# Spare TensorE products in the first two batches, and a re-planned order, in a graph-attention kernel

## The chip, the cores and the metric

The kernel runs on one core of a Trainium2 chip. The metric is the device time of one execution in microseconds. Lower is better. All matrix work is in float32 (some of it in the chip's rounded float32 form for scores).

## The reference

There are 16 batches of 1024 nodes with 256 features and a 1024 x 1024 adjacency of 0 and 1. Each batch goes through two layers, one after the other:

```python
# layer 0: 8 heads of 32
e = einsum('whqd,whkd->whqk', heads(x @ Wq), heads(x @ Wk))
e = where(e >= 0, e, 0.2 * e)
attn = softmax(where(adj > 0, e, NEG), axis=-1)
h = (attn @ heads(x @ Wv)).merge_heads()
o = concat([layernorm(h, g1, b1), x]) @ Wffn.T
x = layernorm(o, g2, b2) + x
# layer 1: two graph attentions, then a feed-forward of 1024
for W, a in ((W1, a1), (W2, a2)):
    Wh = h @ W                                  # h starts as x
    s = leaky_relu(Wh @ a[:256] + (Wh @ a[256:]).T, 0.2)
    h = softmax(where(adj > 0, s, NEG), axis=1) @ Wh
r = layernorm(x + h, g_ln1, b_ln1)
y = layernorm(r + relu(r @ w_ff1 + b_ff1) @ w_ff2 + b_ff2, g_ln2, b_ln2)
```

## The kernel before

**Batches as threads.** Each batch is cut into many small Python generators ("threads"). A thread yields what it needs: an engine for so many nanoseconds (`on`), a buffer of a pool (`take`, `give`), an event (`wait`, `fire`). The class `Order` is a planner that runs when the program is built. It keeps a clock for each engine, picks among the operations that could start within 300 ns (`WINDOW`) the one whose thread has the earliest due time (`aim`), and lets the thread emit the instruction. The order in which instructions are emitted is the order on each engine's queue. Each engine takes its queue strictly in that order, so a plan that is off shows up as waits. The planner also models TensorE's clock: in stretches of 3413 ns, half speed after a stretch that was busy less than 43% (`STRETCH`, `WORK`, `end`).

**Due times.** `SLOT` is the planned time of a batch. `PACE` is the time of two tiles of attention weights. The table `AIM` holds the due times as shares of a slot: when a batch's x, mask and projections come, how fast its heads go (`fast0`, `fast1`, `fast15` for the first, second and last batch; 1 for the others), how far scores may lead (`lead`), and when the rows of the graph layers (`graph`, `graph_step`), the first graph product (`second`), the second one (`normed`) and the feed-forward (`ff`) fall due.

**Layer 0 of a batch.** `project` loads x in four pairs of tiles and turns them (`x_pair`, L351), makes the mask from the adjacency (`mask_part`: DVE at L400, TensorE turns at L409, ACT copies at L413), and projects. `qk_part` computes a half of q or k (L460), splits it into a high and a low part (L463 on ACT, L465 on DVE), and stores both in DRAM through SP's queue (L469). The pool `stage` lets two such parts be in flight. `load_stacks` waits for the four halves of a group of four heads and loads each head's q and k stacks (SP, L543). Then for each head and pair of tiles: scores on TensorE (`all_scores`, L576), scaling by 0.2 on ACT or, in batch 0, DVE (L594, L592), the maximum on DVE (L596), the exponential on ACT (L599), the mask product on POOL (L603), and the product with the values on TensorE (`all_values`, L623). There are 64 such tiles of 128 x 1024 a batch, five buffers `p` and two PSUM buffers for scores.

**The rest of a batch.** `rest` normalizes the heads (L645 to L656, L329 to L345), multiplies with Wffn (L725, L728), and makes the rows of the first graph layer (L757). `attention` makes the graph weights: `first_half` the exponentials of one side, L831 those of the other, `attend` eight rows of 128 x 1024 on DVE (L810, L813) into the one buffer `big`. `second_rows` is the first graph product (L847), `normed_pair` the second (L872, with `as_rows` at L900 adding the residual), `feed_forward` the last stage (L912, L940). The rest of one batch is interleaved with the heads of the next.

**Setup.** `prepare` loads the vectors and small weights through SP's queue, turns and multiplies the weights on TensorE (L1044, L1050), and folds a bias (L1082). Each vector of length 128 c is loaded by `load_cols` (L288) as a tile of 128 partitions and c columns, element by element.

Of the kernel before, what the change touches and what calls it, by code (L numbers as in the profile page):

```python
# [20 lines left out]
P = 128  # L21
# [13 lines left out]
class Order:  # L35
# [18 lines left out]
    def __init__(self, **pools):  # L54
        self.clock = defaultdict(float)
        self.port = 0.0
        self.transfers = 0.0
        self.stretch, self.done, self.half = 0, 0.0, True
        self.pools = {k: [0.0] * n for k, n in pools.items()}
        self.queues = defaultdict(list)  # L60
        self.events = {}
        self.waiting = defaultdict(list)
        self.active = []
        self.made = 0
        self.now = 0.0
        self.busy = defaultdict(float)

    def add(self, thread, aim, ready=0.0):
# [47 lines left out]
    def end(self, engine, t, cost):  # L116
        if engine != "PE":
            return t + cost
        while True:
# [11 lines left out]
            if cost < 0.01:  # L131
                return t

    def run(self):
        while self.active:
            could = []
            for th in self.active:
                costs, shared, delay = th["op"]
                best = None
                for engine, cost in costs.items():  # L140
                    ready = th["ready"]
                    if th.get("last", ())[:2] == (engine, ready):
                        ready -= self.HOP[engine]
                    t = max(self.clock[engine], ready)
                    if shared and engine in ("DVE", "POOL"):
                        t = max(t, self.port)
                    if best is None or t + cost < best[0] + best[2]:
                        best = t, engine, cost
                could.append((best, th))
            first = min(c[0][0] for c in could)  # L150
            (t, engine, cost), th = min((c for c in could if c[0][0] <= first + self.WINDOW),
                                        key=lambda c: (c[1]["aim"], c[1]["no"]))
            if th["op"][1] and engine in ("DVE", "POOL"):

                lead = 100.0 if engine == "DVE" else -100.0
                before = [c for c in could if c[1]["op"][1] and c[0][1] in ("DVE", "POOL")
                          and c[0][1] != engine and c[0][0] + lead < t]
                if before:
                    (t, engine, cost), th = min(before, key=lambda c: (c[1]["aim"], c[1]["no"]))
            costs, shared, delay = th["op"]  # L160
            self.active.remove(th)
            end = self.clock[engine] = self.end(engine, t, cost)
            self.busy[engine] += cost
            if shared and engine in ("DVE", "POOL"):
                self.port = end
            self.now = t
            th["ready"] = end + self.HOP[engine]
            th["last"] = engine, th["ready"]
            if delay:
                self.transfers = max(self.transfers, end + 1000) + 1450 * max(1, round(cost / 500))  # L170
                th["ready"] = max(end + delay, self.transfers + 1200)
                th["last"] = None, 0
            self.step(th, engine)
        stuck = {k: len(v) for k, v in list(self.waiting.items()) + list(self.queues.items()) if v}
        assert not stuck, f"threads that never end: {stuck}"
# [18 lines left out]
def take(pool):  # L194
    return "take", pool
# [29 lines left out]
def unshifted_path(  # L225
# [21 lines left out]
    YW = D + 2  # L247
    NSUM = NT * H + 2 * NT
    NSCORE = 4 * NT
    SLOT = 253e3  # L250
    PACE = SLOT / (H * NT // 2)


    AIM = dict(x=0.818, x_step=0, mask=0.747, mask_step=0.0264, qk0=0.614, qk1=0.898, qk_step=0.0231, v0=0.832,
               v1=0.974, v_step=0.0591, rows=-0.244, rows_step=0.0408, first0=0.12, first1=0.252,
               graph0=-0.009, graph1=0.21, graph_step=0, second=0.355, second_step=0.0335, normed=0.78,
               normed_step=0.026, ff_wait=(None, 0, 1, 0), ff=(0.532, -0.011, 0.487, 0.497), ff_step=0.0386,
               fast0=0.521, fast1=0.85, fast15=0.832, lead=3.15)

    const = ctx.enter_context(tc.tile_pool(name="const", bufs=1))  # L260
    sb = ctx.enter_context(tc.tile_pool(name="sb", bufs=1))
# [21 lines left out]
        nc.sync.dma_start(dst, w.rearrange("(c p) o -> p c o", p=P))  # L283
        return dst

    def load_cols(v, name):
        t = const.tile([P, v.shape[0] // P], FT, name=name)
        nc.sync.dma_start(t, v.rearrange("(c p) -> p c", p=P), allow_slow_non_contiguous=True)  # L288
        return t

    def load_row(v, name):
        t = const.tile([P, v.shape[0]], FT, name=name)
        nc.sync.dma_start(t, bass.AP(tensor=v.tensor, offset=v.offset, ap=[[0, P], [1, v.shape[0]]]))
# [5 lines left out]
    wf2 = const.tile([P, HC, D], FT, name="wf2")  # L299
    w12 = const.tile([P, DC, YW + 2], FT, name="w12")  # L300
    right = const.tile([P, B, 4], FT, name="right")
    k = {}


# [141 lines left out]
    def qk_part(b, g, o, nh):  # L446

        w = (wq, wk)[o]
        cols = slice(nh * HALF, (nh + 1) * HALF)
        for u in range(nh * 2, nh * 2 + 2):  # L450
            yield wait(("xT", b, u))
        yield take("stage")
        yield take("pair")
        yield take("pair")
        yield take("misc")
        pa = misc()
        high, low = (buf([P, HALF], "pair", n) for n in ("high", "low"))
        yield on(PE=1720)
        for dc in range(DC):
            nc.tensor.matmul(pa, w[:, dc, g * P:(g + 1) * P], xTs[b][:, dc, cols],  # L460
                             start=(dc == 0), stop=(dc == DC - 1))
        yield on(ACT=590)
        nc.scalar.copy(high.bitcast(FR), pa)  # L463
        yield on(DVE=690)
        nc.vector.tensor_tensor(low, pa, high, op=OP.subtract)  # L465
        yield give("misc")
        yield load(2)
        for i, part in enumerate((high, low)):
            nc.sync.dma_start(scratch[b, g][o, :, i, cols], part)  # L469
        yield give("pair")  # L470
        yield give("pair")
        yield give("stage")
        yield fire(("qk", b, g, o, nh))

    def project_qk(b, g, t0):
# [130 lines left out]
    def all_values():  # L606
        for b in range(B):
            for h in range(H):
                g, c = h // G, (h % G) * VW
                for u in range(NP):  # L610
                    yield wait(("v", b, g, u))
                v = vs[b, g]
                yield take("acc")
                acc = psum.tile([P, HALF], FT, tag="acc", name="ps_a", bufs=bufs["acc"])
                for d in range(0, NT, GV):
                    for t in range(d, d + GV):
                        yield wait(("p", b, h, t))
                    yield aim(begin[b] + (h * NT + d + 2) / 2 * pace(b), SLOT)
                    yield on(PE=240 + 860 * GV)
                    for t in range(d, d + GV):  # L620
                        p = probs.pop((b, h, t))
                        for nh in range(NH):
                            nc.tensor.matmul(acc[nh * 64:(nh + 1) * 64, :], v[:, t, c:c + 64],  # L623
                                             p[:, nh * HALF:(nh + 1) * HALF],
                                             start=(t == 0), stop=(t == NT - 1))
                    for t in range(GV):
                        yield give("p")
                yield start(after_head(b, h, acc), begin[b] + (h + 1) * NT // 2 * pace(b))
                if h % G == G - 1:
                    yield give("v")  # L630
            yield start(rest(b), work.now)

    def after_head(b, h, acc):
        if h == 0:
# [226 lines left out]
    def normed_pair(b, u, big, y2):  # L861
# [6 lines left out]
        for i, t in enumerate(tiles):  # L868
            for half in range(2):
                yield on(PE=1720)  # L870
                for j in range(half * NT // 2, (half + 1) * NT // 2):
                    nc.tensor.matmul(pa[:, i * D:(i + 1) * D], big[:, j, t * P:(t + 1) * P], y2[:, j, :D],  # L872
                                     start=(j == 0), stop=False)
            yield on(PE=430)
            as_rows(pa, i, x1, i)
        yield fire(("weighed", b, u))
        yield give("pair")
# [48 lines left out]
    def feed_forward(b, u, rT):  # L926
# [9 lines left out]
        for i in range(2):  # L936
            for half in range(2):
                yield on(PE=1720)
                for hc in range(half * HC // 2, (half + 1) * HC // 2):
                    nc.tensor.matmul(pa[:, i * D:(i + 1) * D], hid[hc // 2][:, hc % 2, i * P:(i + 1) * P], wf2[:, hc, :],  # L940
                                     start=(hc == 0), stop=False)
            yield on(PE=430)
            as_rows(pa, i, rT, i)
        for _ in range(HC // 2 + 1):
            yield give("pair")
# [62 lines left out]
    def prepare():  # L1008
# [4 lines left out]
        def part(i, n):  # L1013
            return setup[:, i * 512:i * 512 + DC * n].rearrange("p (c n) -> p c n", c=DC)

        for name, v in (("g1c", g1), ("b1c", b1), ("g2c", g2), ("b2c", b2), ("gl1c", g_ln1), ("bl1c", b_ln1),
                        ("bf1", b_ff1), ("bf2c", b_ff2)):
            yield load(1, 6000)
            k[name] = load_cols(v, name)
        for name, v in (("gl2", g_ln2), ("bl2", b_ln2)):  # L1020
            yield load()
            k[name] = load_row(v, name)
# [24 lines left out]
        def product(wT, dc, by, width):  # L1047
# [3 lines left out]
                                     start=(fc == 0), stop=(fc == DC - 1))  # L1051
            return emit

        for ic in range(2 * DC):
            yield from piece(300, D, wffnT[:, ic, :], flips(wf, ic))
        wTs = []
# [28 lines left out]
        nc.vector.tensor_tensor(k["bf1"], k["bf1"], pa[:, :HC], op=OP.subtract)  # L1085
        yield give("misc")


    with tc.manual_schedule():
        for dst, w in ((wq, Wq), (wk, Wk), (wv, Wv)):  # L1090
            load_w(dst, w)
        work.add(project(0, -SLOT), 0.0)
        work.add(load_stacks(), 0.0)
        work.add(all_scores(), 0.0)
        work.add(all_values(), 0.0)
        work.add(prepare(), 0.5 * SLOT)
        work.run()
# [308 lines left out]
```

## Time and profile before

| | |
|---|---|
| Time of three runs | 4533.11 us in the median, 4531.16 to 4534.94 |
| Profiled span | 4531.4 us, mean granted TensorE clock 0.987 |
| Busy TensorE | 4348.7 us (96%) |
| Busy DVE, ACT, POOL | 3304.5, 2893.6, 2454.6 us |
| L603, mask product on POOL | 1024 of 2177 ns |
| L596, maximum on DVE | 1024 of 1213 ns |
| L623, value products on TensorE | 1019.9 us busy in 4096 |
| L576, scores on TensorE | 631.5 us busy in 2048 |
| L810 and L813, graph rows on DVE | 352.7 and 329.8 us in 256 each |

The profile is one execution. Its busy time of an engine counts the union of that engine's instructions, while the mean of one instruction includes what overlaps with its neighbours; of matmuls, which are pipelined, the busy time divided by the count is the useful figure. A stretch row gives the stretch, its length, the busy time (and number of instructions) of each engine, the TensorE clock granted, and what the DMA engines did.

### The profile page before, as it was taken

The page shows a single profiled execution, that of the slowest core. Times are in us where ns is not written, and L with a number is a line of the kernel's source. Part 1 is how long each engine was busy: PE and PEld are TensorE (multiplying, and loading weights), DVE is VectorE, ACT ScalarE, POOL GpSimd, SP SyncE. Part 2 cuts the span into 40 slices and gives each one's busy share as a digit, 9 for nine tenths or more (in the row PEclk, how much of TensorE's full clock was granted, in tenths as well). Part 3 has the DMA queues.
Part 4 walks back from the last instruction along what each step waited for, and adds up shares of the span by engine and source line. Part 5 has one row for each costly group of instructions (what it writes and reads, how often), then busy time and mean ns, then how long its engine had stood idle before and what let it go on. Part 6 is the DMA issues. An engine that isn't in the chain of part 4 may idle for free.

```text
span 4531.4 us, 57125 instructions
## 1 busy us (share of the span) xinstructions
PE 4348.7 (96%) x20298; PEld 2924.8 (65%) x20298; DVE 3304.5 (73%) x5246; ACT 2893.6 (64%) x4030; POOL 2454.6 (54%) x1544
## 2 busy tenths in 40 slices
PE   6778999999999999999999999999999999999999
PEld 3345666767666676666767666676666767666587
DVE  4766778777787777768777787777768777776854
ACT  4556666666666666666676666666676676666631
POOL 3655565465565545655565565555655565565710
PEclk8899999999999999999999999999999999999999
DMA  5312223222232312323132232322323222231100
GB/s 173 106 49 70 82 70 101 62 79 81 62 98 63 105 54 75 96 59 110 54 89 75 59 98 67 103 64 70 89 64 105 63 86 68 60 99 49 34 22 20
DMA packets 159108, 343.57 MB, mean 76 GB/s; under 512 B 24672, under 2 KB 27232, under 8 KB 158816
## 3 DMA queue, kind: packets, MB, share of 16 engines
q1 hardware_dynamic: 112736, 255.93, 20.0%
q10 hardware_dynamic: 46080, 83.91, 6.2%
q8 instruction: 164, 2.69, 0.2%
q14 instruction: 128, 1.05, 0.1%
HBM read 239.09 MB, written 100.66 MB: 75 GB/s over the span
## 4 chain that ended last, share of the span: by engine, by line
PE 72%; DVE 15%; POOL 5%; issue 4%; ACT 2%; DMA 0%; ACTq 0%; POOLq 0%; SPq 0%; DVEq 0%
PE ps_a L623 16%; PE ps_s L576 10%; PE ps_m L872 8%; PE ps_m L847 8%; PE ps_m L912 7%; PE ps_m L940 7%; DVE att L810 5%; POOL p L603 5%; DVE att L813 5%; PE ps_m L460 3%; DVE p L596 3%; PE ps_m L757 3%; PE ps_m L725 2%; PE ps_m L728 2%; PE ps_m L351 2%
## 5 line engine op out<-in xcount | busy, mean ns | idle before, releaser
L603 POOL TENSOR_TENSOR p<-p,mask 128x1024 f32<-128x1024 f32 x1024 | 2212.3, 2177 | 1654.9 <-ACT p L599 1528.0
L596 DVE TENSOR_TENSOR p<-p,ps_s 128x1024 f32<-128x1024 f32 x1024 | 1209.9, 1213 | 403.0 <-ACT p L594 402.2
L599 ACT ACTIVATE p<-p 128x1024 f32<-128x1024 f32 x1024 | 1081.1, 1058 | 409.7 <-DVE p L596 380.5
L594 ACT ACTIVATE p<-ps_s 128x1024 f32<-128x1024 f32 x993 | 973.6, 1025 | 189.8 <-PE ps_s L576 169.0
L623 PE MATMUL ps_a<-p,v 128*64 128x512 f32 x4096 | 1019.9, 615 | 47.3 <-POOL p L603 45.1
L576 PE MATMUL ps_s<-qs,ks 128*128 128x512 f32 x2048 | 631.5, 428 | 37.2 <-DVE p L596 34.7
L623 PEld LDWEIGHTS ps_a<-p,v 128*64 128x64 f32 x4096 | 246.1, 137 | 536.7 <-issue 384.5
L576 PEld LDWEIGHTS ps_s<-qs,ks 128*128 128x128 f32 x2048 | 352.9, 191 | 331.8 <-DVE p L596 98.3
L872 PE MATMUL ps_m<-y,att 128*128 128x256 f32 x2048 | 483.2, 382 | 16.3 <-ACT v L497 13.6
L940 PE MATMUL ps_m<-wf,hid 128*128 128x256 f32 x2048 | 474.0, 381 | 9.4 <-ACT xT L309 8.7
L912 PE MATMUL ps_m<-rT,wf 128*128 128x256 f32 x2048 | 474.6, 381 | 4.0 <-ACT z L309 4.0
L847 PE MATMUL ps_m<-y,att 128*128 128x258 f32 x2048 | 472.3, 381 | 2.9 <-DVE hn L656 2.9
L872 PEld LDWEIGHTS ps_m<-y,att 128*128 128x128 f32 x2048 | 377.2, 190 | 81.9 <-ACT v L497 16.3
L940 PEld LDWEIGHTS ps_m<-wf,hid 128*128 128x128 f32 x2048 | 379.3, 190 | 78.2 <-issue 15.3
L847 PEld LDWEIGHTS ps_m<-y,att 128*128 128x128 f32 x2048 | 385.9, 190 | 66.7 <-issue 6.0
L912 PEld LDWEIGHTS ps_m<-rT,wf 128*128 128x128 f32 x2048 | 378.6, 191 | 52.7 <-ACT z L309 4.2
L810 DVE SCALAR_TENSOR_TENSOR att<-first,second 128x1024 f32<-128x1024 f32 x256 | 352.7, 1378 | 82.0 <-ACT first L797 82.0
L813 DVE SCALAR_TENSOR_TENSOR att<-mask,att 128x1024 f32<-128x1024 fp8e4 x256 | 329.8, 1288 | 8.7
L818 ACT ACTIVATE y<-y,check 128x258 f32<-128x258 f32 x256 | 130.8, 511 | 299.3 <-DVE check L816 277.7
L334 POOL TENSOR_SCALAR rs<-mv 128x2 f32<-128x2 f32 (+1 forms) x224 | 58.0, 259 | 392.4 <-DVE mv L331 392.3
L400 DVE TENSOR_SCALAR adj_b<-adj_i 128x512 fp8e4<-128x512 int32 x256 | 249.7, 1020 | 15.5 <-DMA adj_i<-in_adj_dram 15.5
L921 ACT ACTIVATE hid<-ps_m,bf 128x256 f32<-128x256 f32 x383 | 163.5, 472 | 130.6 <-PE ps_m L912 102.7
(100 smaller groups left out, 4254.2 us busy)
## 6 DMA issues: line engine op xcount, KB each, us to landing
adj_i<-in_adj_dram ACTq DMA_DIRECT2D x256, 256.0 KB, 3.4
qs<-qk_halves SPq DMA_DIRECT2D x256, 256.0 KB, 4.1
ks<-qk_halves SPq DMA_DIRECT2D x256, 256.0 KB, 5.1
qk_halves<-high SPq DMA_DIRECT2D x128, 256.0 KB, 3.2
qk_halves<-low SPq DMA_DIRECT2D x128, 256.0 KB, 3.7
xr<-in_x_dram ACTq DMA_DIRECT2D x64, 256.0 KB, 2.9
x_kept<-x SPq DMA_DIRECT2D x64, 256.0 KB, 2.0
x<-x_kept SPq DMA_DIRECT2D x64, 256.0 KB, 5.4
```

The lines of the kernel that those rows point to most:

```text
L576: nc.tensor.matmul(ps[i][:, cols], kk[:, t * P:(t + 1) * P], q[:, cols], start=True, stop=True)
L594: nc.scalar.activation(p, ps, AF.Copy, scale=ALPHA)
L596: nc.vector.tensor_tensor(p, p, ps, op=OP.max)
L599: nc.scalar.activation(p, p, AF.Exp)
L603: nc.gpsimd.tensor_tensor(p, p, mask_of(b, t), op=OP.mult)
L623: nc.tensor.matmul(acc[nh * 64:(nh + 1) * 64, :], v[:, t, c:c + 64], p[:, nh * HALF:(nh + 1) * HALF], start=(t == 0), stop=(t == NT - 1))
L810: nc.vector.scalar_tensor_tensor(e, first[:, 0, :], second[:, j:j + 1], first[:, 1, :], op0=OP.mult, op1=OP.max)
L813: nc.vector.scalar_tensor_tensor(e, mask_of(b, j), -1.0, e, op0=OP.mult, op1=OP.mult, accum_out=sums[:, j:j + 1])
L847: nc.tensor.matmul(pa[:, cols:cols + width], big[:, j, i * P:(i + 1) * P], rows[:, j, :width], start=(j == 0), stop=(j == NT - 1))
L872: nc.tensor.matmul(pa[:, i * D:(i + 1) * D], big[:, j, t * P:(t + 1) * P], y2[:, j, :D], start=(j == 0), stop=False)
L912: nc.tensor.matmul(pa[:, i * 2 * P:(i + 1) * 2 * P], wf1[:, dc, hc * P:(hc + 1) * P], rT[:, dc, :], start=(dc == 0), stop=(dc == DC - 1))
L940: nc.tensor.matmul(pa[:, i * D:(i + 1) * D], hid[hc // 2][:, hc % 2, i * P:(i + 1) * P], wf2[:, hc, :], start=(hc == 0), stop=False)
```

## The change

1. `Order.fill` is new. Before the planner gives TensorE an operation that would start later than TensorE's clock by more than 300 ns, it emits 128x128 products of the identity with itself into a buffer of the pool `misc`, each billed at 220 ns, as long as such a buffer is free in the plan. The results are not read. It does so from the start until the last head of batch 1 has been emitted.
2. In batch 0, `qk_part` no longer takes the pool `stage`, so the number of halves in flight is limited only by their other buffers.
3. The eight vectors are loaded as rows of 128 elements, 22 rows in all, into the setup buffer, and one transpose and one copy make the columns from them. The planner's latency for each load goes from 6000 to 3500 ns.
4. The planner's cost of `as_rows` goes from 430 to 230 ns.
5. `SLOT` and all of `AIM` change.

```diff
+    def fill(self, until):
+        while self.spare and until - self.clock["PE"] > self.WINDOW and self.pools["misc"]:
+            if self.pools["misc"][0] > self.clock["PE"]:
+                return
+            self.clock["PE"] = self.end("PE", self.clock["PE"], 220.0)
+            self.spare()
...
+            if engine == "PE":
+                self.fill(t)
             end = self.clock[engine] = self.end(engine, t, cost)
...
-    SLOT = 253e3
+    SLOT = 268e3
...
-    AIM = dict(x=0.818, x_step=0, mask=0.747, mask_step=0.0264, qk0=0.614, qk1=0.898, qk_step=0.0231, v0=0.832,
-               v1=0.974, v_step=0.0591, rows=-0.244, rows_step=0.0408, first0=0.12, first1=0.252,
-               graph0=-0.009, graph1=0.21, graph_step=0, second=0.355, second_step=0.0335, normed=0.78,
-               normed_step=0.026, ff_wait=(None, 0, 1, 0), ff=(0.532, -0.011, 0.487, 0.497), ff_step=0.0386,
-               fast0=0.521, fast1=0.85, fast15=0.832, lead=3.15)
+    AIM = dict(x=0.716, x_step=0, mask=0.525, mask_step=0.019, qk0=0.553, qk1=0.884, qk_step=0.0224, v0=0.804,
+               v1=0.99, v_step=0.0244, rows=-0.105, rows_step=0.0485, first0=0.106, first1=0.114, graph0=0.018,
+               graph1=-0.441, graph_step=0.0071, second=0.315, second_step=0.0335, normed=0.96,
+               normed_step=0.0548, ff_wait=(None, 0, 1, 0), ff=(0.522, 0.109, 0.587, 0.461), ff_step=0.058,
+               fast0=0.581, fast1=0.521, fast15=0.908, lead=4.22)
...
+    columns = const.tile([P, 32], FT, name="columns")
...
-        yield take("stage")
+        if b:
+            yield take("stage")
...
-        yield give("stage")
+        if b:
+            yield give("stage")
...
             yield start(rest(b), work.now)
+            if b == 1:
+                work.spare = None
...
-            yield on(PE=430)
+            yield on(PE=230)
             as_rows(pa, i, x1, i)
...
-            yield on(PE=430)
+            yield on(PE=230)
             as_rows(pa, i, rT, i)
...
-        for name, v in (("g1c", g1), ("b1c", b1), ("g2c", g2), ("b2c", b2), ("gl1c", g_ln1), ("bl1c", b_ln1),
-                        ("bf1", b_ff1), ("bf2c", b_ff2)):
-            yield load(1, 6000)
-            k[name] = load_cols(v, name)
+        for name, v in vectors:
+            n = v.shape[0] // P
+            yield load()
+            nc.sync.dma_start(setup[at:at + n, 2620:2620 + P], v.rearrange("(c p) -> c p", p=P))
+            k[name] = columns[:, at:at + n]
+            at += n
...
+        yield from piece(200, lines, columns[:, :lines],
+                         lambda pt: nc.tensor.transpose(pt[:, :lines], setup[:lines, 2620:2620 + P],
+                                                        ident[:lines, :lines]))
...
+    def spare():
+        nc.tensor.matmul(misc()[:, :P], ident, ident, start=True, stop=True)
...
+        work.spare = spare
```

## The prediction

> **What bounds the kernel now.** I read the page's slices first, then cut the span at the ends of batch 0's heads (272 us), batch 1's first heads (482) and the last heads (4310), and asked for the engines' busy time in each stretch. The page's rows for TensorE, and then the stretches:
>
> ```profile
> PE   6778999999999999999999999999999999999999
> PEclk8899999999999999999999999999999999999999
> ```
> ```profile
> 0.00:46.00 46.00, 28.07 (x135) 17.85 (x135) 10.80 (x23) 13.63 (x29) 1.39 (x12) 0.99 0.66 206
> 46.00:272.00 226.00, 173.53 (x658) 76.11 (x658) 154.89 (x167) 126.34 (x152) 144.47 (x73) 0.84 0.39 107
> 272.00:482.00 210.00, 176.90 (x765) 110.39 (x766) 144.67 (x222) 132.17 (x176) 111.86 (x66) 0.93 0.23 66
> 482.00:600.00 118.00, 111.39 (x528) 73.49 (x527) 87.81 (x150) 80.26 (x118) 66.04 (x45) 0.97 0.28 83
> 600.00:4200.00 3600.00, 3549.14 (x16746) 2404.10 (x16745) 2702.66 (x4290) 2417.04 (x3351) 2030.71 (x1272) 1.00 0.27 77
> 4200.00:4310.00 110.00, 99.94 (x449) 61.23 (x448) 91.78 (x113) 71.14 (x89) 77.97 (x39) 1.00 0.10 27
> 4310.00:4532.00 222.00, 209.71 (x1025) 181.60 (x1023) 111.95 (x284) 53.00 (x119) 22.20 (x40) 0.99 0.06 21
> ```
> The columns are the stretch, its length, busy PE, PEld, DVE, ACT and POOL, the granted clock, DMA. From 600 us on TensorE is busy 98.6% at full clock: it is the bound, and what is not done before 600 us is paid later at the same rate. Before 600 us it idles 18 + 52 + 33 + 7 = 110 us, of the 183 us of the whole span. It also works at a reduced clock there. The same lines by stretch, first L623 and then L576:
>
> ```profile
> 46.00:272.00 226.00, 82.28 (x264) 16.39 (x264) 0.84 0.39 107
> 272.00:482.00 210.00, 48.53 (x192) 11.31 (x192) 0.93 0.23 66
> 600.00:4200.00 3600.00, 830.76 (x3408) 204.42 (x3408) 1.00 0.27 77
> ```
> ```profile
> 46.00:272.00 226.00, 51.12 (x136) 26.82 (x136) 0.84 0.39 107
> 600.00:4200.00 3600.00, 513.59 (x1704) 290.48 (x1704) 1.00 0.27 77
> ```
> L623 takes 312 ns of PE in batch 0 and 244 ns in steady state, L576 376 and 301. The excess is 264 x 68 + 136 x 75 = 28 us, with some 4 us in the other lines 32 us in batch 0; the same sum for L623 in the next stretch is 2 us, with the rest some 8 us up to 600. So 110 us idle and 40 us of slowness can be had before 600 us, 150 in all. In steady state (one batch each 271.5 us, from the ACT exponentials of L831 at 577 and 4107 us, 13 batches apart) only 3.6 us a batch are idle.
>
> Which waits these are, in batch 0 and then in the next stretch:
> ```profile
> PE ps_a L623 <- POOL p L603: 28.8, 26, 3.6
> PE ps_s L576 <- DVE p L596: 8.2, 10, 2.5
> PE ps_m L409 <- DVE adj_b L400: 7.4, 5, 2.5
> ```
> ```profile
> PE ps_s L576 <- DVE p L596: 16.6, 2, 10.4
> PE ps_a L623 <- POOL p L603: 6.2, 8, 1.0
> ```
> Batch 0's 64 weight tiles take 226 us, 3.5 us each, although POOL, with 2.17 us a tile, could do them in 139 us. No engine is full: it is a ring of scores, scaling, maximum, exponential, mask and value product, and TensorE is one of its links. The chain of waits in this stretch puts 16.4% on L623, 12.8% on L576 and 4.1% on L460. The largest single holes of the second stretch come from DVE doing eight graph rows (L810 and L813) in a block from 317 to 340 us while the scores' maximum (L596) waits behind them.
>
> **What the skill says.** The Trainium skill, "TensorE: Matmul & The Clock Gate", Part 1 (The HAM clock gate): the array's clock is at half unless recent activity releases it, decided in free-running windows of about 3.4 us. The trace agrees in kind: 0.50 granted from 46 to 56 us, when PE is busy 4.3 of 10 us, and 1.00 once it is dense. The same page, Part 4, says transposes don't count as activity in the same way; the added product is an ordinary one, and no row here separates the two. "DMA: Bandwidth & Descriptors", Rules for kernel authors: a strided last dimension becomes one descriptor per element. The page here agrees with many small packets (24672 under 512 B), of which the eight vectors would be 7 x 256 + 1024 = 2816.
>
> **The change, part by part.**
> *Spare products.* Until batch 1's heads are done, the planner puts a 128x128 product wherever it believes TensorE idles over 300 ns, one per 220 ns. With 92 us idle from 46 to 600 us that is at most some 400. No row has this product; the nearest, four L351 transposes, take 0.44 us in steady state, so 0.11 us each, to 0.22 at half clock: 45 us to 90 us of PE time, put mostly where PE waits anyway. Gain: the 40 us of slowness. I take 80% as cured, 32 us. Of batch 0's part only what lies on the chain counts in full: PE's roughly 40% of 226 us is 90 us, slow by 32/173 = 18%, so 16 us is the floor if all is cured and 32 the ceiling. Taken: 20 us in all, bounds 0 and 40. Cost: behind a spare product in PE's queue stand the next scores and value products, and the ring waits for these; it also takes a PSUM buffer of the misc ring, so it can wait for an ACT or DVE evacuation. If a tenth of 400 is exposed, that is 4 us; bounds 0 and 56 (all exposed, at 0.14). Taken: -4.
> *First halves without the stage pool.* The first stack loads (SP, L543) start at 35.64 us, behind the fourth pair of half stores at 27.48. Its product (L460) starts at 24.85, though its x was turned by 17.3 and copied by 18.2, since two parts at a time hold the pool until their stores land. Without it, parts three and four can follow at about 18.5 and 20.3: 4.5 to 6 us sooner, on the path, as nothing but that stack starts batch 0. Taken: 5.5, bounds 0 (DMA is already 0.66 full and the misc buffers are three) and 8. The stores of group 1 come sooner on SP's queue too, but one issue is 0.3 us there.
> *Vectors as rows.* Eight SP issues stay eight, of about 0.5 us; 2816 small elements become 22 or so rows of 512 B, and one turn of at most 0.3 us on PE and one copy on ACT or DVE are added. They lie at 54 to 107 us between stack loads that mostly wait for PE. Two of them follow the x loads whose ACT issue stands 5.89 us at 47 us in full DMA engines, but they came after it. Taken: 2, bounds -1 and 6. The setup that waits for them is no wait of PE's but for 2.0 us.
> *Planner's costs.* as_rows is billed 230 instead of 430; the trace has 0.22 us for two (L900). This costs no instruction; with SLOT it only orders. *SLOT 268 for 253* is nearer to the measured 271.5.
> *Aims.* graph_step 0 becomes 0.0071 x 268 = 1.9 us, so graph rows are due one after another and weight tiles can go between: the block of 22 us ends, and with it the holes of 4.65 and 6.24 us at 321 to 341 us. Batch 1's pace goes from 0.85 x 253 = 215 us to 0.521 x 268 = 140 us, so its tiles go ahead of batch 0's rows; batch 0's from 132 to 156, both below the 226 it needs. mask, x and qk are due earlier. Together I give the first 600 us 18 us (10 for the holes, 8 of the other 30 idle), bounds -15 and 40. In steady state: normed goes from 0.78 to 0.96 with a step of 0.055, second from 0.355 to 0.315, ff spread wider. PE's work stays; only its 3.6 us of idle per batch can move: 14 x 3.6 = 50 at best. Taken: 0, bounds -45 and +30. The tail, 25 us idle from 4200 on: 0, within 8.
>
> Sum: 20 - 4 + 5.5 + 2 + 18 = 41.5 us. On the profiled span, 4531.4 - 41.5 = 4489.9. The timed runs lie 1.7 us higher in the median (4533.1, range 4531.2 to 4534.9): 4491.6, so 4492.
>
> **Rivals.**
> 1. *The clock is not what holds batch 0* (or the spare products don't raise it). For it: the chain gives DVE's L596, L592 and L400 36.7%, and DVE is as full as PE. Against it: DVE itself waits 37 us for L576. Then the clock term is near 0 and 41.5 - 20 is left, 4511.
> 2. *The first two batches become dense*: POOL's 139 us leaves up to 87 us in batch 0 alone. If half of it goes (44), the 18 of the next stretch and half of the steady idle (25), that is 87 us: 4446.
> 3. *Slower: the steady batch lengthens.* Place: L872 and the attention behind it. With normed due at 0.96 to 1.12 of a slot (0.78 to 0.86 before), the single big buffer is given back later, the next batch's graph rows start later, and L847 (due at 0.315 on) has to wait where PE is now 98.6% full. Price: 14 us for each us a batch. From 3 us a batch on it eats the 41.5; at 4 us it ends at 4491.6 + 56 = 4548. Against it: rows due late may simply be interleaved, and PE has other work to take. Nothing in the trace before shows slack of this kind, so I can't exclude it.
>
> **How the numbers follow.** Forecast 0.57 (its own range 4462 to 4520), rival 1 0.15, rival 2 0.08, rival 3 0.20. About 9 us (0.2%) is what a measurement of this kernel can tell from no change. Of the forecast nearly all, of rival 1 four fifths and all of rival 2 are faster by more: 0.76. Of the rest 0.06 lies within 0.2% and 0.18 is slower. The range leaves out half of rival 2's side and half of rival 3's: 4447 to 4545.
>
> **What would show it.** Right: granted clock above 0.95 from 46 to 272 us, L623 near 250 ns there, some hundreds of new 128x128 products before 500 us, first L576 at about 40 us instead of 46, batch 0's heads done by about 240, first L831 of batch 1 near 540 instead of 577, and a steady batch of 271 to 272 us. Wrong: a clock as before, the same 3.5 us a tile at full clock (rival 1), or a steady batch over 274 us (rival 3).

## The result, and the profile after

The change made the kernel slower: 4605.89 us in the median (4601.66 to 4610.34) against 4534.02 (4531.16 to 4535.57), a ratio of 1.0159 with a 95% interval of 1.0142 to 1.0177. The prediction said 4492 in a range that ended at 4545. Lines move by some 10 in the changed kernel: the value product is L632 (was L623), the scores L585 (L576), the maximum L605 (L596), the mask product L612 (L603), the normalizing of y L352 (L345), the graph rows L821 and L824 (L810, L813), the exponential that opens a graph attention L842 (L831). The spare product is L1111.

First TensorE's rows of the page in 40 slices, then the stretches that the prediction used, with its columns (window and length, busy us and instructions of PE, PEld, DVE, ACT and POOL, granted clock, DMA share, GB/s):

```profile
PE   7999999999999999999999999999999999999998
PEclk9999999999999999999999999999999999999999
```
```profile
0.00:46.00 46.00, 35.95 (x210) 26.91 (x211) 10.91 (x22) 11.76 (x24) 1.39 (x12) 1.00 0.73 231
46.00:272.00 226.00, 206.21 (x1112) 126.26 (x1110) 159.09 (x175) 130.85 (x156) 148.18 (x75) 0.95 0.36 102
272.00:482.00 210.00, 189.53 (x906) 119.88 (x904) 159.43 (x212) 141.28 (x187) 134.83 (x67) 0.98 0.25 68
482.00:600.00 118.00, 110.18 (x534) 76.07 (x534) 81.96 (x159) 70.14 (x103) 61.28 (x45) 0.94 0.29 88
600.00:4200.00 3600.00, 3505.86 (x16469) 2373.17 (x16466) 2773.70 (x4316) 2344.68 (x3212) 1991.04 (x1251) 1.00 0.27 76
```
The start looks as it was meant to: the idle 110 us before 600 us have become 58, and the granted clock of batch 0 rose from 0.84 to 0.95. But these rows flatter the start, as a product whose result nobody reads counts as busy too: 94 us of this work are such products. The loss stands in the last row: the same 3600 us that held 3549 us of TensorE's work now hold 3506, with DVE 71 us busier.

To date the loss I use the start of the exponential that opens the first graph attention, in batches 1 and 14, before and after. Each line is one instruction: three times its duration in ns (shortest, median, longest), and then its start, first and last, in us:

```profile
L831 ACT ACTIVATE second<-check x1: 198/198/198, 576.8 to 576.8; 128x8 f32<-128x8 f32 x1
L831 ACT ACTIVATE second<-check x1: 205/205/205, 4106.3 to 4106.3; 128x8 f32<-128x8 f32 x1
```
```profile
L842 ACT ACTIVATE second<-check x1: 209/209/209, 572.6 to 572.6; 128x8 f32<-128x8 f32 x1
L842 ACT ACTIVATE second<-check x1: 212/212/212, 4161.1 to 4161.1; 128x8 f32<-128x8 f32 x1
```
Batch 1 gets there 4.2 us sooner. The 13 steady batches take 3588.5 us instead of 3529.5, so 276.0 a batch instead of 271.5: 59 us. From there to the end it is 438.8 us instead of 425.1: 13.7 us. Together -4.2 + 59.0 + 13.7 = 68.5, which is the difference of the spans (4599.9 and 4531.4). The last 13.7 us are not waits: TensorE is idle 25 us there in both, but has 414 us of work against 400. In the runs below that keep the whole mask and have the new SLOT and AIM, this last part takes 435 to 443 us, and in those with the old ones 423 to 431, so the work left over comes with the new due times. Which of them leaves it is not shown.

What TensorE waits for in the steady batches now (total in us, times, longest in us), where before no wait for the scores' maximum stood at all from 577 to 4107 us:

```profile
PE ps_s L585 <- DVE p L605: 31.6, 40, 2.0
PE ps_m L358 <- DVE y L352: 15.0, 6, 2.5
PE ps_m L951 <- ACT xT L316: 8.7, 12, 0.7
PE ps_m L416 <- DVE hn L667: 5.9, 6, 1.0
```
and the DVE group that grew most there, before and after (busy us, mean ns of one, then idle time before it):

```profile
L345 DVE TENSOR_SCALAR y<-y,mv,rs 128x256 f32<-128x256 f32 x208 | 112.5, 572 | 30.2 <-POOL rs L336 29.7
```
```profile
L352 DVE TENSOR_SCALAR y<-y,mv,rs 128x256 f32<-128x256 f32 x210 | 206.3, 1023 | 33.4 <-POOL rs L343 32.6
```
The same step on a tile of the same size, 128x256, takes 1023 ns instead of 572. The mean hides two kinds. Of the 210 steps in the changed kernel 72 began while a mask product of POOL (L612) was running. Each of these took 1.96 to 2.25 us and ended 0.15 us after POOL's product did (0.148 to 0.155). The other 138 took 0.40 to 0.47 us. In the kernel before, only 26 of 208 began so, and these, too, ended 0.15 us after the product. So it is not longer work: the step stands still inside the instruction until POOL's product has ended. One place, in order of time (start and length in us):

```profile
1106.81 2.12 POOL L612 TENSOR_TENSOR p<-p,mask 128x1024 f32<-128x1024 f32 x1
1106.87 2.53 DVE L352 TENSOR_SCALAR y<-y,mv,rs 128x256 f32<-128x256 f32 x2 [1.55 <-POOL rs L343]
1109.22 0.67 PE L358 MATMUL ps_m<-ident,y 128*128 128x128 f32 x4 [2.49 <-DVE y L352]
```
TensorE's turns (transposes) of y stand behind it, idle for 2.49 us. The first row of waits, for the scores' maximum, stands mostly behind two other DVE steps, those that normalize the last result z (L962 and L964). Of its 31.6 us 28.1 come in 30 waits shortly after a z step that was held up in the same way (the z steps end 0.28 us after POOL's product):

```profile
1991.34 4.63 POOL L612 TENSOR_TENSOR p<-p,mask 128x1024 f32<-128x1024 f32 x2 [1.28 <-ACT p L608]
1992.16 1.82 DVE L964 SCALAR_TENSOR_TENSOR z<-z,rs,bl 128x256 f32<-128x256 f32 x1 [0.46 <-DVE z L962]
1993.90 2.35 DVE L962 SCALAR_TENSOR_TENSOR z<-z,mv,gl 128x256 f32<-128x256 f32 x1
1998.49 0.73 PE L585 MATMUL ps_s<-qs,ks 128*128 128x512 f32 x2 [1.94 <-DVE p L605]
```
These z steps were held up in the kernel before as well, and there for longer in the mean (1233 and 1145 ns, now 1147 and 814). New is that the maximum, and with it TensorE, stands behind them.

### The profile page after: what moved, and what is told of

It reads as the page before. It is cut to its first block, busy times and chain, and to the rows that moved or that the text cites. A ratio compares the mean times of both kernels' runs of the same rounds, so it can differ in the third digit from the quotient of the medians.

```text
span 4599.9 us, 58526 instructions
## 1 busy us (share of the span) xinstructions
PE 4427.6 (96%) x21001; PEld 3017.1 (66%) x21001; DVE 3426.2 (74%) x5346; ACT 2859.1 (62%) x3931; POOL 2460.9 (54%) x1544
## 4 chain that ended last, share of the span: by engine, by line
PE 61%; DVE 29%; ACT 3%; POOL 2%; issue 2%; DMA 0%; ACTq 0%; POOLq 0%; DVEq 0%
PE ps_a L632 15%; PE ps_m L858 8%; PE ps_s L585 8%; DVE p L605 8%; PE ps_m L923 5%; PE ps_m L951 5%; DVE att L824 5%; PE ps_m L883 4%; DVE att L821 4%; DVE adj_b L407 3%; PE ps_m L468 3%; DVE y L352 3%; PE ps_m L768 3%; PE ps_m L736 2%; PE ps_m L739 2%; POOL p L612 2%
## 5 line engine op out<-in xcount | busy, mean ns | idle before, releaser
L612 POOL TENSOR_TENSOR p<-p,mask 128x1024 f32<-128x1024 f32 x1024 | 2230.2, 2194 | 1385.0 <-ACT p L608 1227.6
L605 DVE TENSOR_TENSOR p<-p,ps_s 128x1024 f32<-128x1024 f32 x1024 | 1211.4, 1213 | 429.3 <-ACT p L603 426.9
L603 ACT ACTIVATE p<-ps_s 128x1024 f32<-128x1024 f32 x994 | 973.3, 1021 | 247.3 <-PE ps_s L585 229.9
L632 PE MATMUL ps_a<-p,v 128*64 128x512 f32 x4096 | 1005.7, 611 | 8.1 <-POOL p L612 7.9
L585 PE MATMUL ps_s<-qs,ks 128*128 128x512 f32 x2048 | 632.0, 427 | 51.9 <-DVE p L605 51.4
L585 PEld LDWEIGHTS ps_s<-qs,ks 128*128 128x128 f32 x2048 | 350.0, 190 | 352.9 <-DVE p L605 138.5
L632 PEld LDWEIGHTS ps_a<-p,v 128*64 128x64 f32 x4096 | 249.0, 137 | 475.0 <-issue 384.4
L883 PE MATMUL ps_m<-y,att 128*128 128x256 f32 x2048 | 482.1, 380 | 3.6 <-DVE low L473 3.6
L858 PE MATMUL ps_m<-y,att 128*128 128x258 f32 x2048 | 476.7, 381 | 1.4 <-DVE low L473 1.4
L858 PEld LDWEIGHTS ps_m<-y,att 128*128 128x128 f32 x2048 | 384.5, 189 | 80.7 <-issue 16.7
L883 PEld LDWEIGHTS ps_m<-y,att 128*128 128x128 f32 x2048 | 374.9, 189 | 60.4 <-issue 6.7
L821 DVE SCALAR_TENSOR_TENSOR att<-first,second 128x1024 f32<-128x1024 f32 x256 | 348.6, 1362 | 66.9 <-ACT first L808 66.9
L824 DVE SCALAR_TENSOR_TENSOR att<-mask,att 128x1024 f32<-128x1024 fp8e4 x256 | 355.7, 1389 | 8.7
L352 DVE TENSOR_SCALAR y<-y,mv,rs 128x256 f32<-128x256 f32 x256 | 235.0, 959 | 41.6 <-POOL rs L343 40.7
L407 DVE TENSOR_SCALAR adj_b<-adj_i 128x512 fp8e4<-128x512 int32 x256 | 250.5, 1023 | 13.1 <-DMA adj_i<-in_adj_dram 13.1
```

The costliest lines, as they stand in the source:

```text
L585: nc.tensor.matmul(ps[i][:, cols], kk[:, t * P:(t + 1) * P], q[:, cols], start=True, stop=True)
L603: nc.scalar.activation(p, ps, AF.Copy, scale=ALPHA)
L605: nc.vector.tensor_tensor(p, p, ps, op=OP.max)
L612: nc.gpsimd.tensor_tensor(p, p, mask_of(b, t), op=OP.mult)
L821: nc.vector.scalar_tensor_tensor(e, first[:, 0, :], second[:, j:j + 1], first[:, 1, :], op0=OP.mult, op1=OP.max)
L824: nc.vector.scalar_tensor_tensor(e, mask_of(b, j), -1.0, e, op0=OP.mult, op1=OP.mult, accum_out=sums[:, j:j + 1])
```

## The experiments

The steady batch below is always (start of the exponential in batch 14 minus that in batch 1) / 13. Theories A to E, D1 and D2 are those of the expectations; each is named where it is first expected.

**Aims, products, or any new order.** Four kernels: the new SLOT and AIM alone on the kernel before; the change with SLOT and AIM of before; the change without spare products; the spare products alone.

```diff
# no_spares: the change without this line
-        work.spare = spare
```


> Only SLOT and AIM of the change on the kernel before. Theory A (the new due times lengthen the steady batch, 276.2 us against 271.5, over 13 batches): the steady batch is 275 to 277 us and the time 4590 to 4620. Theory B (the spare products, 94 us of TensorE time, are what costs): the steady batch may move, but the time stays at 4520 to 4550. Theory C (any new order costs, since the due times of before fit only their own plan): between the two, and the other re-planned kernels of this set are slower than before as well.

> The change with SLOT and AIM of before. Theory A: the steady batch is back at 271 to 273 us and the time at 4505 to 4540. Theory B: 4560 to 4610, as the 94 us of spare products stay. Theory C: a steady batch of 273 to 276 and 4550 to 4590.

> The change without its spare products (none is ever emitted), all else as changed. Theory A: the steady batch stays at 275 to 277 us; batches 0 and 1 lose the raised clock; the time is 4600 to 4635. Theory B: 4520 to 4570, 40 or more below the change.

> Only the spare products on the kernel before. Theory A: steady batch 271 to 273 us, granted clock from 46 to 272 us raised from 0.84 to 0.95, time 4500 to 4540. Theory B: 4560 to 4600. Theory C: steady batch over 273 us and over 4550.

| | time, ratio to before (interval) | steady batch |
|---|---|---|
| aims_only | 4804.7, 1.0611 (1.0592 to 1.0629) | 290.0 |
| old_aims | 4794.0, 1.0581 (1.0564 to 1.0599) | 290.6 |
| no_spares | 4788.3, 1.0564 (1.0546 to 1.0582) | 291.0 |
| spares_only | 4532.1, 1.0001 (0.9992 to 1.0010) | 271.4 |

Neither theory A nor B held. The first three, which mix the change with the kernel before, are 182 to 272 us slower than either of the two kernels. Theory C is right in one thing, that the other re-planned kernels are slower too, though not in its numbers: due times fit the plan for which they were set, and a change elsewhere can throw the steady order over. It isn't any re-planning, though: spares_only keeps the steady batch. Its 53 us of spare products, of which none stands ahead of the first scores (the first comes at 111.0 us), are in sum neither gain nor loss, although the clock of batch 0 goes from 0.84 to 0.91 and L634 (the value product) from 312 to 275 ns.

**One planner cost.** The prediction priced the new cost of as_rows at nothing.

```diff
# rows230, on the kernel before, in normed_pair and feed_forward
-            yield on(PE=430)
+            yield on(PE=230)
```


> The kernel before with one number changed: the planner's cost of as_rows is 230 instead of 430 as in the change; no instruction is added or removed. If a cost of the planner is only an order of equals, as the prediction priced it: steady batch 271 to 272.5 us, time 4525 to 4545. If the due times fit only the plan for which they were set (theory C): steady batch 280 us or more, time over 4640, like the other three re-planned kernels.

4892.2 us, ratio 1.0796 (1.0778 to 1.0814), 298.5 us a batch: the slowest of the kernels with the whole mask, from a number that emits no instruction. Of the 27.0 us a batch, 17.0 are idle time of TensorE, and 10.0 are longer busy time for the same work (16449 records against 16432) at a granted clock of 0.97 instead of 1.00. The DVE row that changed most is the mask step of the graph rows:

```profile
L813 DVE SCALAR_TENSOR_TENSOR att<-mask,att 128x1024 f32<-128x1024 fp8e4 x208 | 496.5, 2387 | 7.2
```
It was 1259 ns in the kernel before. In rows230 131 of the 208 steps were held up by a mask product of POOL that ran when they began. They took 3.03 to 3.21 us and ended 1.08 us after it; the others took 1.22 to 1.23 us. Across the orders this mean goes roughly with the batch: 1259 and 271.5, 1286 and 276.0 (the change), 1850 and 290.0 (aims_only), 1858 and 291.0 (no_spares), 2221 and 290.6 (old_aims), 2387 and 298.5. That is a likeness, not a test.

**POOL's mask products.** The steps that stand still (L352, L962, L964, and L813, which is L824 in the changed kernel) are among those that the planner marks `shared`, between DVE and POOL. It keeps one common clock for these, so in a plan they never overlap; in the run they do wherever the plan is off. So: the same plans to the instruction, and half of each mask product.

```diff
# half_mask_after, half_mask_before and half_mask_rows230, in weights
-        nc.gpsimd.tensor_tensor(p, p, mask_of(b, t), op=OP.mult)
+        nc.gpsimd.tensor_tensor(p[:, :HALF], p[:, :HALF], mask_of(b, t)[:, :HALF], op=OP.mult)
```


> The change with the plan as changed, but POOL multiplies only the left half of each weight tile by the mask, the right half stays unmasked: 1.07 us instead of 2.17, so what waits for POOL[...] waits half as long. Theory D (the steady batch is longer because the new order puts DVE's normalizing and graph rows against POOL's mask products): the steady batch falls from 276 to 268 to 271 us, the normalizing of y from 1023 to under 600 ns; time 4500 to 4540. Theory E (the new order makes TensorE wait for DVE's queue as such): 273 to 276 us, time 4560 to 4600.

> The kernel before with the same half left unmasked, as the control. Steady batch: 270 to 271.5 us, as only 3.6 us of a batch are idle TensorE. In batch 0, if POOL holds the ring of tiles, its heads end 40 us or more earlier (225 instead of 268); if DVE and TensorE hold it, under 20 us. Time 4470 to 4525.

> The kernel before with the planner's cost of as_rows at 230, and POOL masking only the left half of each weight tile. If POOL's products[...] are what makes a re-planned batch 298.5 us (the mask step of a graph row, L813, takes 2387 ns there against 1259): 270 to 280 us and L813 under 1400 ns. If the order itself leaves TensorE without work: over 288 us.

With half the mask left out, the program runs `general_path` after the first path, so the total times (17783, 17766 and 17936 us) say nothing; the batches are those of the first path. The steady batch is 268.3 us in the changed order and 268.3 in the order of before, where 270 to 271.5 had been expected: the whole excess of 4.5 us is gone. TensorE is busy for all but 1.8 us of it in both orders. So the excess needs POOL's whole products; through which DVE step it comes, this run does not tell. The y step and the wait for the maximum, in the changed order with half a mask:

```profile
L352 DVE TENSOR_SCALAR y<-y,mv,rs 128x256 f32<-128x256 f32 x210 | 115.0, 589 | 13.4 <-POOL rs L343 13.1
PE ps_s L585 <- DVE p L605: 3.5, 12, 0.4
```
In the order with the cost of 230 the batch falls from 298.5 to 281.3 us and L813 from 2387 to 1796 ns; I had expected more (270 to 280, under 1400 ns). Against the control with half a mask (268.3) the excess falls from 27.0 to 13.0 us, so 14 of the 27 are POOL's doing. The rest may come from the half products that are left, as 135 mask steps are still held up by them, or from the order itself. In batch 0 the control shows POOL as a link, but not the only one: its graph attention opens at 273.9 instead of 308.2 us, 34 us sooner, where 40 or more had been set as the sign that POOL holds it.

**Is the y step the place?** First the same values on ACT (Identity with a scale and a bias), in the changed plan.

```diff
# y_on_act_after, in normalized, for y alone
+                nc.vector.scalar_tensor_tensor(nb, mv[:, :, 0], -1.0, rs, op0=OP.mult, op1=OP.mult)
...
-            nc.vector.tensor_scalar(row, src, mv[:, i, 0:1], rs[:, i:i + 1], op0=OP.subtract, op1=OP.mult)
+            nc.scalar.activation(row, src, AF.Identity, scale=rs[:, i:i + 1], bias=nb[:, i:i + 1])
```


> The change with its plan, but the two normalizing steps of each y pair (1023 ns each on DVE in the steady batch, 572 before the change) run on ACT from one small DVE step (the same values). Theory D (in the changed order[...] DVE's queue behind them holds TensorE): steady batch from 276 to 270 to 273 us, time 4520 to 4570, and TensorE's waits for the scores' maximum (31.6 us) and for y (15.0) mostly gone. Theory E (any DVE or ACT delay of that kind only moves elsewhere): 275 us or more, time 4590 to 4640.

4652.4 us, ratio 1.0264 (1.0247 to 1.0281), 279.3 us a batch: worse than the change. Now ACT stands in its queue before these steps (115.7 us of waits for the small DVE step nb), with exponentials behind them. The wait moved, so the run told nothing of the place. The batch fits theory E, that such a delay only moves, though the time lies beyond its range. So the step was left out, in both orders.

```diff
# no_y_after, no_y_before, in normalized, for y alone: the step is not issued
+            if skip:
+                continue
```


> The change with its plan, but the two normalizing steps of each y pair are left out (y goes on as it is), so DVE has 16 steps a batch less, of 1023 ns each. If these steps are the place where the change loses its 4.7 us a batch (theory D1): steady batch 269 to 272 us, at most 1 us above the control, and 4510 to 4560. If it is lost elsewhere in the order too (D2): 273 to 276 us, 2 us or more above the control.

> The control: the kernel before with the same steps left out, 572 ns each. TensorE is idle 3.6 us of a batch, so the steady batch is 269.5 to 271.5 us by either theory, and the time 4500 to 4535.

Without it the changed order takes 4560.9 us and 273.1 us a batch, the control 4527.9 and 271.5. So the y step is worth 2.9 of the 4.5 us in the changed order and nothing in the other. The rest, 1.6 us a batch, lies between the 1 us that D1 allowed and the 2 us of D2, so a part is lost elsewhere. TensorE's wait for the scores' maximum is still 30.7 us there, 28.1 of them behind z steps that were held up, as with the y step in place. So the z steps are the likely place of that rest. They were not left out alone, and this is read from the traces, not tested.

**The spare products in their own plan.** The planner counts them, the kernel doesn't issue them, so that all else keeps its order.

```diff
# muted (late_spares returns only for the first 62)
     def spare():
-        nc.tensor.matmul(misc()[:, :P], ident, ident, start=True, stop=True)
+        return
```


> The change with the plan as changed, to the instruction, but its spare products not issued (the planner still counts them). Theory B' (the spare products stand in the way at the start: 124 records of them run from 36.55 to 50.7 us ahead of the first scores, whose stacks land at some 43): the first scores start at 42 to 44 us, and the time is 5 to 15 us below the change's 4606. Theory A' (they raise the clock, and that is worth more): 10 to 40 us above it. Both: the steady batch stays at 276 us, since the order there is the same.

> The change with its plan, but without the first 62 spare products, those that stand ahead of the first scores; the other 289 are issued. If only those 62 cost anything: first scores at 40 us as in the run with all of them muted, and the raised clock of batch 0 is a gain on top: 4580 to 4590, below the muted run's 4595. If the later ones are exposed as well: 4595 to 4602, between the two.

Muted: 4595.4 us (1.0132, 1.0115 to 1.0148). Without the first 62: 4599.0 (1.0154, 1.0137 to 1.0171). With all 351: 4605.9. So all of them together cost some 10 us, and the later ones show no gain. The intervals of these three overlap, so neither the sum nor the split between the 62 and the rest is sure from them alone; the trace shows the 62 plainly. TensorE in the changed kernel, from 35 us on, and then the first scores of the changed and of the muted kernel:

```profile
36.44 0.28 PE L416 MATMUL ps_m<-ident_b,adj_b 128*128 128x128 bf16 x2
36.55 14.39 PE L1111 MATMUL ps_m<-ident 128*128 128x128 f32 x124
50.70 1.17 PE L585 MATMUL ps_s<-qs,ks 128*128 128x512 f32 x4
```
```profile
L585 PE MATMUL ps_s<-qs,ks x8: 393/434/765, 50.7 to 56.1; 128*128 128x512 f32 x8
```
```profile
L585 PE MATMUL ps_s<-qs,ks x16: 390/475/796, 40.3 to 59.2; 128*128 128x512 f32 x16
```
In the muted kernel the scores start at 40.3 us, so what they read had landed by then; in the changed kernel the run of spare products goes on to 50.7. 10 us of them stood in front of scores that could have run. The plan had that gap longer than it was. For the later ones, late_spares and muted start their scores at the same 40.3 us, but batch 0's graph attention opens at 308.7 us with the products and at 302.9 without, although the granted clock of batch 0 is 0.95 with them and 0.92 without.

**The small parts.**

```diff
# stage_only, in qk_part on the kernel before (give likewise)
-        yield take("stage")
+        if b:
+            yield take("stage")
```
vectors_only is the diff of part 3 of the change on the kernel before.

> The kernel before with only the stage pool lifted in batch 0. As the prediction priced it: first scores at some 40.5 us instead of 46.0, time 4525 to 4531. Rival: the halves of group 1 now stand on SP's queue ahead of the first stacks and crowd the same transfers, so that batch 0's heads end no sooner: time 4533 to 4555. Theory D says of it: steady batch 271 to 272 us and the mask step of the graph rows (L813) at 1260 ns, unless this start, too, throws the later order over, in which case over 1800 ns and over 285 us.

> The kernel before with only the vectors loaded as rows and turned. As predicted: 2 us gained, 4528 to 4534. Rival: the turn and the earlier setup come between the tiles of batch 0 and cost 3 to 10 us: 4536 to 4545. Theory D as for the run with only the stage pool lifted.

stage_only: 4526.5 us, ratio 0.9991 (0.9982 to 1.0000). vectors_only: 4530.2, ratio 0.9998 (0.9989 to 1.0007), which can't be told from nothing. The steady batch stays at 271.5 and 271.6. The medians gain 5.5 and 1.8 us, close to the predicted 5.5 and 2, but the interval of the first reaches 1.0000 too. The way was not the predicted one: first scores start at 44.5 us with the stage pool lifted, 1.5 sooner, not 5.5, though batch 0's graph attention opens at 303.8 instead of 308.2. The fourth pair of half stores starts at 23.79 instead of 27.48 us. But eight pairs now stand ahead of the first stack load on SP's queue instead of six, and that load, which follows directly on the last of them, starts at 34.27 instead of 35.64.

**The parts of the start together**, with SLOT, AIM and the cost of 430 as before; then the same plan without the 75 spare products that stand ahead of the first scores, and without any.

```diff
# three_parts, on the change: SLOT and AIM of before, and
-            yield on(PE=230)
+            yield on(PE=430)
```


> The change without what reaches the steady batches: spare products, rows of vectors and the lifted stage pool, with SLOT, AIM and the planner's cost of as_rows as before. If the three parts add up (0, 2 and 5.5 us) and the steady batch stays at 271.5: 4520 to 4528. If they don't, or the order is thrown over as in the other re-planned kernels: over 4535.

> As three_parts (4544), in the same plan, without the 75 spare products that stand ahead of the first scores. If those alone cost it: first scores at 41 to 43 us instead of 53.5, time 4530 to 4535. If the later spare products gain by the raised clock: below 4530.

> As three_parts, in the same plan, with no spare product issued. If the later spare products are a gain (batch 0 is the only place, with a granted clock of 0.96 against some 0.88): slower than three_late by 3 to 15 us. If they are neither: the same within 3 us. If they stand in the way there too: faster than three_late.

| | time, ratio to before (interval) | first scores | batch 0's graph attention opens |
|---|---|---|---|
| three_parts | 4544.3, 1.0023 (1.0014 to 1.0032) | 53.5 | 314.8 |
| three_late | 4533.9, 1.0002 (0.9994 to 1.0010) | 42.0 | 301.5 |
| three_muted | 4528.0, 0.9986 (0.9980 to 0.9993) | 41.7 | 298.1 |

In a plan whose steady batch is as before (271.5 to 271.7 us), the answer is clear of noise, for the later products narrowly. The spare products before the first scores cost 10 us, the later ones 6, and the other two parts are a gain of 5 to 6 us. three_muted is the one complete kernel of these runs whose interval of the ratio lies wholly below 1.

## Why the prediction was wrong

**"In steady state ... Taken: 0" failed, and its 59 us are most of the miss.** It is the term of the sum that gave no time to the order of 14 batches, because TensorE's work stays. The work nearly did stay (268.7 us a batch busy against 267.6). The idle time went from 3.9 to 7.3 us a batch. Together that is 4.5 us a batch, 59 us over the 13 batches; the tail, taken as 0, added 13.7. It is the outcome of rival 3, whose price of 14 us for each us a batch was near (59 us for 4.5); the time is still longer than its 4548, as the start gave 4.2 us where 41.5 were counted. Its place was wrong. L847 doesn't wait for the buffer `big`; L858 and L883, as the two products are called now, wait 5 us in all over the whole run. In its place the runs show DVE steps that are held up by POOL's mask products: the y steps, with TensorE's turns behind them (2.9 us a batch, by leaving them out), and the z steps, with the scores' maximum behind them (by the traces alone). The sign of that was in the profile before: L345 had 572 ns in the mean for y but 407 in the median, L400 1027 in the mean with 0.42 us in the first 40 us, both `shared`. A step whose mean is well above its usual time waits for somebody inside the instruction, and a new order changes for how long and who stands behind it.

**"This costs no instruction; with SLOT it only orders" failed as a price of nothing.** On the kernel before, this number alone makes 360 us. An order is not free where an engine's queue is strict and its steps stand still behind another engine's. In the changed kernel the due times were set together with it, and no run shows what it costs there.

**"Taken: 20 us in all" and "Taken: -4" failed in their sum, a gain of 16 us that was a loss of some 10 to 16.** The granted clock and the matmuls came nearly as forecast: 0.95, L632 at 70.1/272 = 258 ns and L585 at 324, against 312 and 376. But not all of that is the products' doing, as the same plan without them (muted) has a clock of 0.92 and L632 at 291. The step that failed is the pass from there to the end. Batch 0 gains nothing by it in spares_only (its graph attention opens at 308.7, before 308.2), and in late_spares it opens 5.8 us later than in muted. That fits rival 1, that the clock does not hold batch 0. The runs show only the sum of what the clock gave and what the products cost; the two were not measured apart. The price of a product was too low as well: a row of the trace is half of such a product, and 351 products leave 702 rows (705 in the three stretches below, as a row across a border counts twice; they show the instructions of L1111 alone: window and length, TensorE's busy time and rows, the weight loads' own, granted clock, DMA share, GB/s):

```profile
0.00:46.00 46.00, 9.39 (x82) 9.25 (x83) 1.00 0.73 231
46.00:272.00 226.00, 58.94 (x443) 54.90 (x441) 0.95 0.36 102
272.00:482.00 210.00, 25.35 (x180) 23.29 (x180) 0.98 0.25 68
```
That is 94 us in all, 0.27 us each, where the prediction took 0.11 to 0.22 from turns, which are one row each. And the exposed part was not a tenth: 62 products stood for 10 us in front of the first scores alone.

**"Taken: 5.5" for the first halves and "Taken: 2" for the vectors came out in size when each part ran alone.** The first is luck in part, since the way was another one: six pairs of stores stood ahead of the first stack load, not four, and lifting the pool put two more ahead of it. The second can't be told from nothing. In the changed kernel both are buried, as its first scores start at 50.7.

**"Together I give the first 600 us 18 us" was not reached.** Batch 1 opens its graph attention 4.2 us sooner in all and 15.5 sooner in muted (561.3). So the aims and the small parts together gave 15.5, where 25.5 were counted, and the products took 11 back.

What stays open: whether the z steps are the whole of the 1.6 us a batch that the changed order loses beside the y steps, which due times bring the two into their new places, and what makes the 13 us in rows230 that half a mask didn't remove.

## What to carry to other kernels

When every engine's order is planned, a cost, a due time and an added filler are one thing: undo one part of a tuned set and the time says nothing of that part, unless the order of the rest is held fixed, as by issuing or not issuing within the same plan. Price a new order by the steps that already take longer than their shortest case, since they show which queue stands still behind which engine, and then ask what of the busiest engine's work will stand behind them: the z steps lost less in the mean after the change, but TensorE now waited for what came behind them. A filler put where a plan expects idle time must be shorter than the true gap, above all in front of the instruction that starts everything.

## What the runs showed of the hardware

- Some DVE steps that begin while a 128x1024 mask product of POOL runs end a fixed time after it. In the changed kernel's steady batches this was 0.15 us for the y step (72 of 72, 26 of 26 before) and 0.28 for the z steps (58 of 58); for the 131 long mask steps of rows230 it was 1.08. With POOL's products half as wide the mean y step went from 1023 to 589 ns. The longer time is inside the instruction, not before it, so the waits of DVE don't show it.
- Not every DVE instruction does this: the maximum over scores (L605) began under such a product 360 times there and took 1.20 to 1.22 us, as it did elsewhere.
- A float32 product of 128x128 is two rows of the trace (62 issued, 124 recorded), a float32 turn is one.
- In one plan, with the first scores at 40.3 us in both runs, the spare products behind these scores raised the granted clock of batch 0 from 0.92 to 0.95 and shortened its value product from 291 to 262 ns (muted and late_spares). Batch 0 did not end sooner by it: its graph attention opened at 308.7 us with these products and at 302.9 without.
